# Projections packed as 128 columns and two 64-column halves, with a new order, in a four-layer kernel bound by TensorE

## The chip, the cores and the metric

The kernel runs on one core of a Trainium2 chip. The metric is the time of one execution in device microseconds (us). A kernel's time is the median of its runs; a profile describes one execution of its own.

## The reference

64 images of 96 channels and 28x28 pixels, in fp32, go through four layers in turn. Cut to what matters:

```python
# layer 0, B=64, C=96, HID=576, E=4 experts
rw   = softmax(relu(mean_hw(x) @ r_w1.T + r_b1) @ r_w2.T + r_b2)      # routing weights of an image
h    = silu(bn1(einsum('oc,bchw->bohw', exp_w, x)))                   # 96 -> 576
h    = silu(bn2(depthwise_5x5(h, einsum('be,eckl->bckl', rw, dw_w)))) # a kernel of its own for each image
h    = h * sigmoid(silu(mean_hw(h) @ se_w1.T + se_b1) @ se_w2.T + se_b2)
x    = x + bn3(einsum('boc,bchw->bohw', einsum('be,eoc->boc', rw, pw_w), h))   # 576 -> 96
# layers 1 and 3 (each with its own weights)
h    = relu(bn1(conv1x1(x, w1)));  h = relu(bn2(depthwise_3x3(h, wd)))
x    = x + bn3(conv1x1(h, w3))                                        # 576 -> 96
# layer 2, on the four 14x14 quadrants of an image
q    = group_norm(quadrants(x)); a = silu(conv1x1(q)); u = silu(depthwise_3x3(conv1x1(q)))
y    = selective scan of u in four directions, 16 states a channel
x    = x + channel_gate(a * group_norm(y))
```

The last step of layers 0, 1 and 3, 576 channels to 96 with the batch norm folded into the weights, is here called the projection.

## The kernel before

**Stages.** The images go through a software pipeline. One slot (`slot`) holds the scans of layer 2 for image t (`mamba`), layer 1 of image t+1, layer 0 of image t+2 and layer 3 of image t-1. There are 64 slots; `opening` comes before them and the last layer 3 after them.

**A convolution layer.** `expand` multiplies 96 channels to 576 in tiles of 128 channels (matmuls of 392 columns, L725; the last 64 channels as two 64-column matmuls, L755). ScalarE evicts each tile with batch norm and activation into one of two border tiles (L709), and a DMA from ScalarE's queue stores it to `ex` in DRAM (L742). A border tile can be filled again when its store has landed. `load` reads shifted rows back from `ex` into `rep` (SyncE's queue), `depthwise` runs the depthwise convolution as matmuls of 32 columns (L835), and ScalarE evicts into nine tiles `acc` of 128 partitions and 392 columns (L845). Such a tile g holds 64 channels; half of its partitions carry the even rows of the image (parity 0), half the odd rows (parity 1).

`project` sums over the nine tiles. There are two PSUM banks, one for each parity. The weights of a group g and a parity o are 96 columns whose rows of the other parity are zero, so that a group takes two matmuls over the same `acc` (L872), 18 in all. For layer 0 the weights `wp` are made for each image in `squeeze_excite`: matmuls mix the experts, and VectorE multiplies by the gate (L994). For layers 1 and 3 they are constants that `fold_bn3` scaled before the loop. VectorE then adds each bank and the bias to x in SBUF, one instruction for each parity (`add`, L876).

**Layer 2.** `head` normalizes (`group_norm`, whose matmuls are L1075, L1071 and L1072), projects (L1119, L1162) and runs the small convolution (L1141, L1173). `scans` has ScalarE make decays (L1269) and copy `du` (L1279, one buffer), VectorE make products (L1291) and scan them in two directions (L1296, L1301), GpSimd add and weigh them (L1248), and TensorE collect them into `y` (L1223). `tail` normalizes, gates and adds to x.

**The order.** The whole program is straight-line code. `Plan` collects operations with an engine, a cost in us, buffers, keys and a due time, and `run` places them one after another on modelled engines: among those that can start soon it takes the one with the earliest due time. The due times come from a slot's length T, from where an operation stands in its slot, and from a table of offsets, `DUE`, with one entry for each kind of operation. The result is one fixed order of instructions for each engine, and each engine runs its own in that order. The costs only decide the order, not what the chip does. Where TensorE would have been idle for long in the model, `idle` puts matmuls on zeros (L539) to keep its clock up. PSUM has four banks of the pool `ps`, one for `y`, one for `du` and two for the products.

Of the kernel before, what the change touches and what calls it, by code (L numbers as in the profile page):

```python
# [15 lines left out]
P = 128  # L16
C = 96
# [235 lines left out]
class Plan:  # L253
# [7 lines left out]
    LAND = 0.7  # L261
    ALONE = 130e3
# [60 lines left out]
    def run(self, start=0.0):  # L323
# [23 lines left out]
        while left:  # L347
# [42 lines left out]
            o.behind = None  # L390
# [82 lines left out]
class Kernel:  # L473
    T = 145.0
# [13 lines left out]
        wp=(1, [P, 2, NG, C]),  # L488
# [90 lines left out]
    def fold_bn3(self, row, w3):  # L579

        k = w3.shape[1]
        self.nc.vector.tensor_tensor(w3, w3, row.rearrange("p (a o) -> p a o", a=1).to_broadcast([P, k, C]), ALU.mult)
# [12 lines left out]
    def setup(self, fold, banks):  # L595
# [22 lines left out]
        for layer, c in ((1, c1), (3, c3)):  # L618
# [4 lines left out]
            self.fold_bn3(self.row_of(banks, s3, eye, f"fold_row{layer}"), c("w3"))  # L623
# [75 lines left out]
    def expand(self, d):  # L699
# [17 lines left out]
        for t in range(4):  # L717
# [3 lines left out]
            for h in range(2):  # L721
                ps = pl.buf("ps")

                def mm(ps=ps, t=t, h=h):
                    nc.tensor.matmul(  # L725
                        ps()[:, :HALF], w1[:, t * P : t * P + P], x[:, h * HALF : (h + 1) * HALF], start=True, stop=True
                    )

                pl.op(PE, 0.72, mm, r=d["keys"], w=[ps], after=[("pad", i, h)])
                pl.op(  # L730
                    ACT, 0.68, lambda ps=ps, t=t, h=h, pad=pad: evict(pad[:, :, 1 + 7 * h : 8 + 7 * h, 2:30], ps, t),
                    r=[ps], w=[("pad", i, h)], table=d["table"],
                )
# [37 lines left out]
        pl.op(ACT, 0.68, lambda: evict(pad[:, :, :, 2:30], ps, 4), r=[ps], w=["hpad"], table=d["table"])  # L771
# [14 lines left out]
    def load(self, d, u):  # L786
# [18 lines left out]
        if layer == 0:  # L805
            pl.op(POOL, 1.3, spread, r=[d["kern"]], w=[wd])
# [7 lines left out]
    def depthwise(self, d, u):  # L814
# [41 lines left out]
    def project(self, d):  # L856
# [3 lines left out]
        if d["layer"] == 0:  # L860
            wp = self.squeeze_excite(d)
            terms = lambda o, g: (wp()[:, o, g], accs[g]())
        else:
            w3, wp = d["c"]("w3"), "none"
            terms = lambda o, g: (w3[:, NG * o + g], accs[g]())
        banks = [pl.buf("ps") for o in range(2)]

        def mm(lo):
            for g in range(lo, lo + 3):
                for o in range(2):  # L870
                    w, a = terms(o, g)
                    nc.tensor.matmul(banks[o]()[:C, :HALF], w, a, start=(g == 0), stop=(g == NG - 1))  # L872

        def add(o):
            xs = d["x"].rearrange("c (r o w) -> c o r w", o=2, w=28)[:, o]
            nc.vector.scalar_tensor_tensor(  # L876
                xs, banks[o]()[:C, :HALF].rearrange("c (r w) -> c r w", w=28), d["b3"], xs, ALU.add, ALU.add
            )

        for lo in range(0, NG, 3):  # L880
            pl.op(PE, 0.67 * 6, lambda lo=lo: mm(lo), r=[*(accs[lo : lo + 3] if lo else accs), wp], w=banks)
        for o in range(2):
            pl.op(DVE, 0.65, lambda o=o: add(o), r=[banks[o], *d["keys"]], w=d["keys"])

    def routing(self, d):
# [6 lines left out]
        pl.op(DVE, 0.97, lambda: nc.vector.tensor_reduce(rw()[:C, 9:10], d["x"], AX.X, ALU.add), r=d["keys"], w=[rw])  # L892
# [5 lines left out]
            ACT, 0.35,  # L898
# [15 lines left out]
        pl.op(DVE, 0.6, top, w=[pt, rw])  # L914
        pl.op(ACT, 0.21, lambda: nc.scalar.activation(pt()[:, :E], pt()[:, :E], AF.Exp), w=[pt], table=EXP)

        def weights():
# [5 lines left out]
        pl.op(DVE, 0.75, weights, r=[pt], w=[rw])  # L923
        pl.op(
            ACT, 0.3, lambda: nc.scalar.activation(mix(), c("smask"), AF.Copy, scale=rw()[:, 10:11]), r=[rw], w=[mix]
# [7 lines left out]
        pl.op(ACT, 0.58, lambda: nc.scalar.copy(kern(), pk()[:96, :360]), r=[pk], w=[kern])  # L933

    def squeeze_excite(self, d):
# [16 lines left out]
        pl.op(ACT, 0.6, hidden, r=[ps], w=[sc], table=SILU)  # L952
# [27 lines left out]
        pl.op(DVE, 0.2, lambda: nc.vector.tensor_tensor(v(), ps()[:, 8 : 8 + NG], c("se_b2"), ALU.add), r=[ps], w=[sc])  # L980
# [8 lines left out]
        pl.op(ACT, 0.92, gate, w=[sc], table=SILU)  # L989
        for lo, hi, bank, acc in banks:  # L990
            for o in range(2):
                pl.op(
                    DVE, 0.58,
                    lambda o=o, lo=lo, hi=hi, acc=acc: nc.vector.tensor_tensor(  # L994
                        wp()[:, o, lo:hi],
                        acc(),
                        sc()[:, o * NG + lo : o * NG + hi].rearrange("p (g a) -> p g a", a=1).to_broadcast([P, hi - lo, C]),
                        ALU.mult,
                    ),
                    r=[sc, bank], w=[wp],  # L1000
                )
# [48 lines left out]
    def group_norm(self, key, imgs):  # L1050
# [23 lines left out]
        pl.op(DVE, 1.05, stats, r=key, w=[gs])  # L1074
        pl.op(PE, 0.25, lambda: nc.tensor.matmul(ps()[:C, :2], ones, mv()[:, :, 0], start=True, stop=True), r=[gs], w=[ps])  # L1075
        pl.op(ACT, 0.7, deviations, r=[ps], w=[gs])
        pl.op(PE, 0.4, second, r=[gs], w=[ps2])
        pl.op(ACT, 0.24, lambda: nc.scalar.activation(inv(), ps2()[:C, :2], AF.Identity, bias=self.eps), r=[ps2], w=[gs])
# [17 lines left out]
    def head(self, q):  # L1096
# [14 lines left out]
        pl.op(ACT, 1.1, norm, r=[gs, q["xkey"]], w=["hn"])  # L1111
# [21 lines left out]
        pl.op(ACT, 0.9, keep, r=banks, w=["p2"])  # L1133
        ps = pl.buf("ps")

        def taps(ps=ps):
# [14 lines left out]
            ACT, 0.6,  # L1151
# [14 lines left out]
            ACT, 0.6, lambda ps=ps: nc.scalar.activation(flat(a), ps()[:C, :HALF], AF.Silu, bias=c("p1_b")),  # L1166
# [10 lines left out]
        pl.op(ACT, 0.5, lambda: nc.scalar.copy(self.bc, ps2()[C:, :HALF]), r=[ps2], w=["bc"])  # L1177
        pl.op(ACT, 0.36, lambda: nc.scalar.dma_start(self.bcd[i2], self.bc), r=["bc"], w=[("bcd", i2)], nbytes=50176, land=2.2)
        pl.op(
            ACT, 0.58,  # L1180
# [3 lines left out]
        pl.op(POOL, 1.02, lambda: nc.gpsimd.tensor_tensor(inner(2), inner(0), u, ALU.mult), r=["dd0", q["ukey"]], w=["dd2"])  # L1184
        pl.op(
            POOL, 0.9,
# [16 lines left out]
    def scans(self, q, at):  # L1203
# [49 lines left out]
        for k in range(2):  # L1253
# [6 lines left out]
            for j in range(J):  # L1260
# [5 lines left out]
                def decay(fs=fs, d=dd[j], k=k, j=j):  # L1266
# [9 lines left out]
                pl.op(ACT, 1.88, decay, r=[dd[j]], w=[("decay", n)], table=EXP, due=at(i) - 9.0)  # L1276
                du = pl.buf("du")
                pl.op(
                    ACT, 0.5, lambda du=du, d=dd[j]: nc.scalar.copy(du()[:, :HALF], d()[:, 2]), r=[dd[j]], w=[du], due=at(i) - 3.0  # L1279
                )  # L1280
                for o in range(2):
# [4 lines left out]
                    def products(du=du, B=B, o=o):  # L1286
# [6 lines left out]
                    pl.op(DVE, 1.0, products, r=[du, B], w=["b"])  # L1293
                    pl.op(
                        DVE, 1.78,
# [4 lines left out]
                        DVE, 1.78,  # L1300
# [5 lines left out]
                    if not o:  # L1306
                        first = g
                        pooled(1.88, [h], g, ALU.add, h, g)
# [4 lines left out]
                    pooled(1.88, [h, g], yc, ALU.add, h, g, turned=True)  # L1313
                pooled(1.73, [first], yc, ALU.add, yc, first)
                pooled(1.88, [Cs], yc, ALU.mult, yc, c=Cs)
# [4 lines left out]
    def tail(self, q):  # L1320
# [6 lines left out]
            DVE, 0.65,  # L1327
# [11 lines left out]
        pl.op(ACT, 0.57, affine, w=[gs])  # L1339
# [13 lines left out]
        pl.op(ACT, 1.1, norm, r=[gs, q["ukey"]], w=[pa])  # L1353

        def gated():
# [4 lines left out]
        pl.op(DVE, 0.95, gated, r=[q["akey"], pa], w=[q["ukey"], cz])  # L1360
        pl.op(PE, 0.25, lambda: nc.tensor.matmul(pc()[:MID, :2], c("ca1"), cz()[:, :2], start=True, stop=True), r=[cz], w=[pc])
        pl.op(
            ACT, 0.25,
# [12 lines left out]
        pl.op(ACT, 0.58, sigmoid, r=[pd], w=[cz], table=EXP)  # L1376
# [12 lines left out]
        pl.op(DVE, 0.82, gate, r=[q["ukey"], cz], w=[q["xkey"]], lock=True)  # L1389
# [130 lines left out]
```

## Time and profile before

| | |
|---|---|
| median of 3 runs | 9306.1 us (9301.3 to 9313.9) |
| profiled execution, its time | 9312.2 us |
| its span, first to last instruction | 9310.4 us |
| TensorE busy | 8870.7 us (95%), mean granted clock 0.965 |
| VectorE busy | 7772.0 us (83%) |
| GpSimd busy | 6778.1 us (73%) |
| ScalarE busy | 6345.8 us (68%) |
| DMA engines, mean | 218 GB/s |

How to read the lines shown below. The page's first part gives for each engine its busy time, its share of the span and its instructions; PE is TensorE, PEld its weight loads, DVE VectorE, ACT ScalarE, POOL GpSimd, SP SyncE. A line of the view of stretches has the stretch in us from the start, its length, the busy time of PE, PEld, DVE, ACT and POOL with the number of instructions, the granted TensorE clock as a share of full speed, the busy share of the DMA engines, and GB/s. A line of a group has the source line, engine, operation, the tiles written and read, shapes and count, then busy us and mean ns of one, then the idle time of the engine just before them and what ended it. A line of the timeline has start, duration, engine, source line, operation and, in brackets, the idle time before it and what ended that. An fp32 matmul has two records. Line numbers are those of the kernel before; from L539 on, those of the kernel after are 5 to 17 higher.

### The profile page before, as it was taken

What the parts mean: (1) busy time and instruction counts of PE and PEld (TensorE: products, weight loads), DVE (VectorE), ACT (ScalarE), POOL (GpSimd) and SP (SyncE); (2) the same over time, 40 slices, a digit from 0 to 9 for tenths busy, and PEclk for the clock granted to TensorE, in tenths of its full rate; (3) what the DMA queues carried; (4) which work ended last, traced back from release to release, by engine and by line L of the source; (5) the groups of instructions that cost most, each with busy time, mean ns of one, the idle gap of its engine ahead of it and who ended that gap; (6) DMA issues with size and microseconds to landing.
All of it is one profiled execution on the core that took longest, in us unless ns stands there. A gap on an engine that the chain in (4) does not pass through costs nothing. (4 is left out here: it accounts for less than half of the span.)

```text
span 9310.4 us, 198515 instructions
## 1 busy us (share of the span) xinstructions
PE 8870.7 (95%) x78114; PEld 4120.6 (44%) x78114; DVE 7772.0 (83%) x7806; ACT 6345.8 (68%) x10934; POOL 6778.1 (73%) x4445
## 2 busy tenths in 40 slices
PE   7899999999999999999999999999999999999997
PEld 3344444444444444444444444444444444444443
DVE  1888888888888888888888888888888888888886
ACT  3667767767667677667677676676676676776763
POOL 2777777777777777777777777777777777777775
PEclk9899999999999999999999999999999999999998
DMA  6688888888888888888888888888888888888884
GB/s 174 185 213 231 223 220 225 227 222 220 224 226 219 221 229 221 215 229 224 219 225 227 223 222 225 224 220 222 228 221 222 227 222 215 230 223 220 225 227 105
DMA packets 1063983, 2029.93 MB, mean 218 GB/s; under 512 B 114065, under 2 KB 890001, under 8 KB 1062673
## 3 DMA queue, kind: packets, MB, share of 16 engines
q1 hardware_dynamic: 810576, 1520.44, 66.6%
q10 hardware_dynamic: 252480, 496.79, 15.4%
q8 instruction: 624, 10.22, 0.5%
q14 instruction: 303, 2.47, 0.1%
HBM read 1499.83 MB, written 516.95 MB: 217 GB/s over the span
## 5 line engine op out<-in xcount | busy, mean ns | idle before, releaser
L835 PE MATMUL ps<-rep,wd 64*32 64x392 f32 (+1 forms) x50688 | 3609.0, 521 | 38.8 <-DMA rep<-ex 14.9
L1301 DVE TENSOR_TENSOR_SCAN g<-decay,b 128x788 f32<-128x788 f32 x1536 | 2755.1, 1794 | 324.8 <-ACT decay L1269 190.1
L1296 DVE TENSOR_TENSOR_SCAN h<-decay,b 128x788 f32<-128x788 f32 x1536 | 2721.4, 1772 | 0.0
L835 PEld LDWEIGHTS ps<-rep,wd 64*32 64x32 f32 (+1 forms) x50688 | 1491.4, 110 | 1822.9 <-issue 1596.4
L1248 POOL TENSOR_TENSOR yc<-h,g 128x784 f32<-128x784 f32 x768 | 1436.9, 1871 | 1095.9 <-DVE h L1296 657.6
L1291 DVE TENSOR_TENSOR b<-du,B 128x784 f32<-128x784 f32 x1536 | 1505.0, 980 | 675.9 <-ACT du L1279 605.8
L845 ACT ACTIVATE acc<-ps,l_bn2b,l_bn2s 128x392 f32<-128x392 f32 x1728 | 1124.2, 674 | 1338.1 <-PE ps L835 1311.3
L1248 POOL TENSOR_TENSOR g<-h,g 128x784 f32<-128x784 f32 x768 | 1425.7, 1856 | 801.4 <-DVE h L1296 800.6
L872 PE MATMUL ps<-acc,blob 128*96 128x392 f32 x4608 | 1602.3, 498 | 4.7
L1248 POOL TENSOR_TENSOR yc<-yc,C 128x784 f32<-128x784 f32 x768 | 1426.5, 1857 | 55.2
L1269 ACT ACTIVATE decay<-dd,A 128x784 f32<-128x784 f32 x1536 | 1372.5, 943 | 38.0 <-DVE h L1296 14.4
L1248 POOL TENSOR_TENSOR yc<-yc,g 128x784 f32<-128x784 f32 x768 | 1318.1, 1716 | 45.9
L725 PE MATMUL ps<-x,blob 96*128 96x392 f32 x3072 | 1186.5, 518 | 22.3 <-ACT border L709 9.5
L709 ACT ACTIVATE border<-ps,l_bn1b,l_bn1s 128x392 f32<-128x392 f32 x1536 | 976.0, 677 | 220.0 <-DMA ex<-border 109.1
L872 PEld LDWEIGHTS ps<-acc,blob 128*96 128x96 f32 x4608 | 725.8, 163 | 755.8 <-issue 635.3
L588 POOL TENSOR_TENSOR wd<-kern,blob 96x640 f32<-96x640 f32 x576 | 753.6, 1317 | 163.1 <-PE ps L835 85.1
L1269 ACT ACT_TABLE_LOAD x439 | 563.2, 1283 | 334.7 <-issue 178.6
L725 PEld LDWEIGHTS ps<-x,blob 96*128 96x128 f32 x3072 | 536.7, 191 | 547.5 <-ACT acc L845 79.7
L872 PE MATMUL ps<-acc,wp 128*96 128x392 f32 x2304 | 771.8, 493 | 0.6 <-ACT a L1166 0.6
L872 PEld LDWEIGHTS ps<-acc,wp 128*96 128x96 f32 x2304 | 376.4, 163 | 383.7 <-issue 373.6
L1279 ACT COPY du<-dd 128x392 f32<-128x392 f32 x768 | 374.2, 487 | 219.0 <-DVE b L1291 124.3
L1223 PE MATMUL y<-yc,blob 128*32 128x392 f32 x3072 | 398.1, 502 | 29.8 <-POOL yc L1248 29.8
(144 smaller groups left out, 6599.8 us busy)
## 6 DMA issues: line engine op xcount, KB each, us to landing
rep<-ex SPq DMA_DIRECT2D x4032, 224.0 KB, 5.1
ex<-border ACTq DMA_DIRECT2D x512, 480.0 KB, 5.5
dd<-ddd SPq DMA_DIRECT2D x384, 588.0 KB, 7.2
ex<-border ACTq DMA_DIRECT2D x256, 512.0 KB, 5.1
B<-bcd SPq DMA_DIRECT2D x256, 392.0 KB, 4.3
C<-bcd SPq DMA_DIRECT2D x256, 392.0 KB, 4.8
wd<-taps SPq DMA_DIRECT2D x512, 192.0 KB, 6.7
ddd<-dd ACTq DMA_DIRECT2D x128, 441.0 KB, 3.5
```

Source lines behind the costliest of these rows:

```text
L588: self.nc.gpsimd.tensor_tensor(out, taps.rearrange("k (n a) -> k n a", a=1).to_broadcast([k, n, cb]), mask.rearrange("k (a c) -> k a c", a ...
L709: nc.scalar.activation(dst, ps()[:, :HALF].rearrange("p (r o w) -> p o r w", o=2, w=28), d["func"], bias=bias[:, t : t + 1], scale=scale[: ...
L725: nc.tensor.matmul(ps()[:, :HALF], w1[:, t * P : t * P + P], x[:, h * HALF : (h + 1) * HALF], start=True, stop=True)
L835: nc.tensor.matmul(ps()[32 * b : 32 * b + 32, :HALF], wd()[64 * h : 64 * h + lanes, at : at + 2 * CB], rep()[64 * h : 64 * h + lanes, b, : ...
L845: nc.scalar.activation(acc(), ps()[:, :HALF], d["func"], bias=bias[:, at : at + 1], scale=scale[:, at : at + 1], **kw)
L872: nc.tensor.matmul(banks[o]()[:C, :HALF], w, a, start=(g == 0), stop=(g == NG - 1))
L1223: nc.tensor.matmul(y()[32 * j : 32 * j + 32, :HALF], c("sel"), ys[j]()[:, 2 * u : 2 * u + 2], start=(k == 0 and u == 0), stop=(k == 1 and ...
L1248: nc.gpsimd.tensor_tensor(*vs, op)
L1269: nc.scalar.activation(fs[:, :, u, :, :SEQ], d()[:, :2].rearrange("p o (i l) -> p o i l", i=2), AF.Exp, scale=self.A[:, at : at + 1],)
L1291: nc.vector.tensor_tensor(out, v, w, ALU.mult)
L1296: lambda h=h, ff=ff: nc.vector.tensor_tensor_scan(flat(h()), ff, b, 0.0, ALU.mult, ALU.add),
L1301: lambda g=g, ff=ff: nc.vector.tensor_tensor_scan(flat(g())[:, ::-1], ff[:, ::-1], b[:, ::-1], 0.0, ALU.mult, ALU.add),
```

## The change

A group's two matmuls of 96 columns become one of 128 columns and two of 64 columns over half of the pixels each. The 128 columns hold all 96 outputs of parity 0 and the outputs 64 to 95 of parity 1. The outputs 0 to 63 of parity 1 are made by two matmuls of 64 columns and 196 pixels, which lie in the two column halves of the array and write the two halves of the second bank's partitions. VectorE adds four pieces to x in place of two: 96 and 32 partitions of the first bank, and twice 64 partitions of the second. The weights are packed to match: `w3` and `wp` have 192 columns for each group; the gating of parity 1 in layer 0 takes two instructions a bank, and the fold takes three instructions a layer in layers 1 and 3.

The order is planned anew. `T` goes from 145 to 134, the table `DUE` is another one, many modelled costs are lower (some are shown), and the model gives a result a short lag after its engine is free.

```diff
-    out = np.zeros((4, 2, CB, 2, NG, C), np.float32)
-    for o in range(2):
-        out[:, o, :, o] = w3.reshape(4, 2, CB, NG, C)[:, o]
-    p.add("w3", out.reshape(P, 2 * NG, C))
+    w3 = w3.reshape(4, 2, CB, NG, C)
+    out = np.zeros((4, 2, CB, NG, 2 * C), np.float32)
+    out[:, 0, :, :, :C] = w3[:, 0]
+    out[:, 1, :, :, C:P] = w3[:, 1, :, :, 64:]
+    out[:, 1, :, :, P:] = w3[:, 1, :, :, :64]
+    p.add("w3", out.reshape(P, NG, 2 * C))
...
 DUE = (
-    71, -2, 48, -17, 58, 181, 21, -12, 9, -37, -2, 21, 37, -23, 1, -16, 19, -12, 30, -17, 33, -40, 12, -8, -30, -60,
...
+    3, -600, 26, 3, -7, 47, 39, 26, 30, 0, -27, -34, 26, 4, 10, -8, 4, 15, 102, 0, 101, -7, -12, -94, -208, -19, -99,
...
+    LAG = {PE: 0.0, DVE: 0.1, ACT: 0.1, POOL: 0.05, SP: 0.0}
...
+            else:
+                end += lag
...
-                    d.ready = max(d.ready, end + (self.HOP[d.engine] if d.engine != e or o.nbytes else 0.0))
+                    d.ready = max(d.ready, end + (self.HOP[d.engine] if d.engine != e or o.nbytes else min(lag, 0.1)))
...
-    T = 145.0
+    T = 134.0
...
-        wp=(1, [P, 2, NG, C]),
+        wp=(1, [P, NG, 2 * C]),
...
-            self.fold_bn3(self.row_of(banks, s3, eye, f"fold_row{layer}"), c("w3"))
+            row = self.row_of(banks, s3, eye, f"fold_row{layer}")
+            for lo, hi, out in ((0, C, 0), (64, C, C), (0, 64, P)):
+                self.fold_bn3(row[:, lo:hi], c("w3")[:, :, out : out + hi - lo])
...
-                ACT, 0.88 if sums else 0.68, lambda ps=ps, acc=acc, h=h: evict(ps, u if sums else 2 * u + h, acc),
+                ACT, 0.67 if sums else 0.57, lambda ps=ps, acc=acc, h=h: evict(ps, u if sums else 2 * u + h, acc),
...
             for g in range(lo, lo + 3):
-                for o in range(2):
-                    w, a = terms(o, g)
-                    nc.tensor.matmul(banks[o]()[:C, :HALF], w, a, start=(g == 0), stop=(g == NG - 1))
+                w, a, kw = weights()[:, g], accs[g](), dict(start=(g == 0), stop=(g == NG - 1))
+                nc.tensor.matmul(banks[0]()[:, :HALF], w[:, :P], a, **kw)
+                for h in range(2):
+                    nc.tensor.matmul(
+                        banks[1]()[64 * h : 64 * h + 64, :SEQ], w[:, P:], a[:, h * SEQ : h * SEQ + SEQ], **kw
+                    )
...
+        def first():
+            add(xs(0), banks[0]()[:C, :HALF], 0, C)
+            add(xs(1)[64:], banks[0]()[C:, :HALF], 64, C)
+
+        def second():
+            for h in range(2):
+                add(xs(1)[:64, 7 * h : 7 * h + 7], banks[1]()[64 * h : 64 * h + 64, :SEQ], 0, 64)
+
         for lo in range(0, NG, 3):
-            pl.op(PE, 0.67 * 6, lambda lo=lo: mm(lo), r=[*(accs[lo : lo + 3] if lo else accs), wp], w=banks)
-        for o in range(2):
-            pl.op(DVE, 0.65, lambda o=o: add(o), r=[banks[o], *d["keys"]], w=d["keys"])
+            pl.op(PE, 3.0, lambda lo=lo: mm(lo), r=[*(accs[lo : lo + 3] if lo else accs), wp], w=banks)
+        pl.op(DVE, 1.02, first, r=[banks[0], *d["keys"]], w=d["keys"])
+        pl.op(DVE, 0.64, second, r=[banks[1], *d["keys"]], w=d["keys"])
...
+            def gated(o, lo=lo, hi=hi, acc=acc):
+                for a, b, out in ((0, C, 0),) if o == 0 else ((64, C, C), (0, 64, P)):
+                    v = sc()[:, o * NG + lo : o * NG + hi].rearrange("p (g a) -> p g a", a=1)
+                    nc.vector.tensor_tensor(
+                        wp()[:, lo:hi, out : out + b - a], acc()[:, :, a:b], v.to_broadcast([P, hi - lo, b - a]), ALU.mult
+                    )
...
-                pl.op(ACT, 1.88, decay, r=[dd[j]], w=[("decay", n)], table=EXP, due=at(i) - 9.0)
+                pl.op(ACT, 1.68, decay, r=[dd[j]], w=[("decay", n)], table=EXP, due=at(i) - 9.0)
...
-                    pl.op(DVE, 1.0, products, r=[du, B], w=["b"])
+                    pl.op(DVE, 0.9, products, r=[du, B], w=["b"])
```

More of the change, by code (lines that the diff above doesn't have):

```diff
@@ L389, in run @@
             free[e] = end = t + cost
-            o.behind = None
+            o.behind, lag = None, self.LAG[e]
             if o.lock:
@@ L805, in load @@
         if layer == 0:
-            pl.op(POOL, 1.3, spread, r=[d["kern"]], w=[wd])
+            pl.op(POOL, 1.27, spread, r=[d["kern"]], w=[wd])
         else:
@@ L897, in routing @@
         pl.op(
-            ACT, 0.35,
+            ACT, 0.25,
             lambda: nc.scalar.activation(
@@ L912, in top @@
             nc.vector.tensor_scalar(lg, lg, m, None, ALU.subtract)
-        pl.op(DVE, 0.6, top, w=[pt, rw])
-        pl.op(ACT, 0.21, lambda: nc.scalar.activation(pt()[:, :E], pt()[:, :E], AF.Exp), w=[pt], table=EXP)
+        pl.op(DVE, 0.52, top, w=[pt, rw])
+        pl.op(ACT, 0.13, lambda: nc.scalar.activation(pt()[:, :E], pt()[:, :E], AF.Exp), w=[pt], table=EXP)
         def weights():
@@ L921, in weights @@
             nc.vector.scalar_tensor_tensor(rw()[:, :4], lg, m, c("emask"), ALU.mult, ALU.mult, accum_out=rw()[:, 10:11])
-        pl.op(DVE, 0.75, weights, r=[pt], w=[rw])
+        pl.op(DVE, 0.55, weights, r=[pt], w=[rw])
         pl.op(
-            ACT, 0.3, lambda: nc.scalar.activation(mix(), c("smask"), AF.Copy, scale=rw()[:, 10:11]), r=[rw], w=[mix]
+            ACT, 0.27, lambda: nc.scalar.activation(mix(), c("smask"), AF.Copy, scale=rw()[:, 10:11]), r=[rw], w=[mix]
         )
@@ L932, in routing @@
         pl.op(PE, 0.65, kernels, r=[mix], w=[pk])
-        pl.op(ACT, 0.58, lambda: nc.scalar.copy(kern(), pk()[:96, :360]), r=[pk], w=[kern])
+        pl.op(ACT, 0.4, lambda: nc.scalar.copy(kern(), pk()[:96, :360]), r=[pk], w=[kern])
     def squeeze_excite(self, d):
@@ L950, in hidden @@
             nc.scalar.activation(sc()[:n4, 3 * NG + 1 :], c("zmask"), AF.Copy, scale=z())
-        pl.op(ACT, 0.6, hidden, r=[ps], w=[sc], table=SILU)
+        pl.op(ACT, 0.5, hidden, r=[ps], w=[sc], table=SILU)
         def excite():
@@ L987, in gate @@
                 nc.scalar.activation(sc()[:, o * NG : o * NG + NG], v(), AF.Identity, bias=par, scale=par)
-        pl.op(ACT, 0.92, gate, w=[sc], table=SILU)
+        pl.op(ACT, 0.82, gate, w=[sc], table=SILU)
         for lo, hi, bank, acc in banks:
-            for o in range(2):
[L992 to L1001, printed above, removed]
+            def gated(o, lo=lo, hi=hi, acc=acc):
[4 more added lines that the diff above has]
+                    )
+            for o in range(2):
+                pl.op(DVE, 0.52 + 0.1 * o, lambda o=o, gated=gated: gated(o), r=[sc, bank], w=[wp])
         return wp
@@ L1109, in norm @@
                 )
-        pl.op(ACT, 1.1, norm, r=[gs, q["xkey"]], w=["hn"])
+        pl.op(ACT, 0.9, norm, r=[gs, q["xkey"]], w=["hn"])
         banks = [pl.buf("ps"), pl.buf("ps")]
@@ L1131, in keep @@
             nc.scalar.copy(self.p2[:, 2], banks[1]()[:, :224])
-        pl.op(ACT, 0.9, keep, r=banks, w=["p2"])
+        pl.op(ACT, 0.7, keep, r=banks, w=["p2"])
         ps = pl.buf("ps")
@@ L1150, in head @@
         pl.op(
-            ACT, 0.6,
+            ACT, 0.5,
             lambda ps=ps: nc.scalar.activation(
@@ L1299, in scans @@
                     pl.op(
-                        DVE, 1.78,
+                        DVE, 1.7,
                         lambda g=g, ff=ff: nc.vector.tensor_tensor_scan(
@@ L1326, in tail @@
         pl.op(
-            DVE, 0.65,
+            DVE, 0.53,
             lambda: nc.vector.scalar_tensor_tensor(flat(u), flat(u), self.D4, q["y"]()[:C, :HALF], ALU.mult, ALU.add),
@@ L1351, in norm @@
                 )
-        pl.op(ACT, 1.1, norm, r=[gs, q["ukey"]], w=[pa])
+        pl.op(ACT, 0.9, norm, r=[gs, q["ukey"]], w=[pa])
         def gated():
@@ L1387, in gate @@
                 )
[L1389 removed]
+        pl.op(DVE, 0.64, gate, r=[q["ukey"], cz], w=[q["xkey"]], lock=True)
     def mamba(self, t, base, span, more):
```

59 lines of the change are left out of this document (29 added, 30 removed), and 8 rows, old and new, of the table DUE.

## The prediction

> **What bounds the kernel now.** I read the page first, then the busy time of three slots, then TensorE's groups with their idle time, then the timeline around the longest wait. Page and stretches:
>
> ```profile
> PE 8870.7 (95%) x78114; PEld 4120.6 (44%) x78114; DVE 7772.0 (83%) x7806; ACT 6345.8 (68%) x10934; POOL 6778.1 (73%) x4445
> ```
> ```profile
> 4620.04:4762.23 142.19, 137.38 (x1219) 64.11 (x1219) 120.60 (x122) 98.94 (x172) 105.47 (x69) 0.97 0.85 222
> 4762.23:4902.43 140.20, 136.15 (x1218) 63.56 (x1218) 119.72 (x121) 99.38 (x172) 105.53 (x69) 0.98 0.85 225
> 4902.43:5044.24 141.81, 136.12 (x1219) 63.15 (x1219) 123.03 (x123) 99.19 (x172) 105.50 (x69) 0.97 0.86 223
> ```
>
> The three stretches are one slot each (from one L1075 to the same one a slot later): 141.4 us, TensorE busy 136.6 of it, VectorE 121.1, GpSimd 105.5, ScalarE 99.2. TensorE is the bound, with 4.8 us idle a slot; VectorE has 20.3. But 136.6 is not all work: the clock column says 0.97. Where idle time and lost clock come from:
>
> ```profile
> L872 PE MATMUL ps<-acc,blob 128*96 128x392 f32 x4608 | 1602.3, 498 | 4.7
> ...
> L872 PE MATMUL ps<-acc,wp 128*96 128x392 f32 x2304 | 771.8, 493 | 0.6 <-ACT a L1166 0.6
> ...
> L1162 PE MATMUL ps<-hn,blob 96*96 96x392 f32 x256 | 115.1, 531 | 34.1 <-ACT p L1131 31.8 <-ACT acc L845 2.0 <-ACT p L1130 0.3
> ...
> L1075 PE MATMUL ps<-gs,blob 96*96 96x2 f32 x512 | 84.6, 235 | 228.7 <-ACT border L709 226.8 <-DVE gs L1063 1.9
> ```
> ```profile
> 4613.10 0.52 ACTq L742 DMA_DIRECT2D ex<-border  x1
> ...
> 4619.31 1.25 ACT L709 ACTIVATE border<-ps,l_bn1b,l_bn1s 128x392 f32<-128x392 f32 x2 [2.58 <-DMA ex<-border]
> ...
> 4620.04 0.48 PE L1075 MATMUL ps<-gs,blob 96*96 96x2 f32 x2 [4.63 <-ACT border L709]
> ```
> ```profile
> 4608.00:4615.30 7.30, 7.30 (x36) 3.27 (x28) 2.57 (x6) 5.69 (x9) 0.00 (x0) 1.00 1.04 255
> 4615.30:4620.00 4.70, 0.11 (x1) 0.00 (x0) 3.17 (x2) 2.12 (x4) 0.00 (x0) 0.90 0.73 254
> 4620.00:4628.70 8.70, 8.57 (x70) 5.07 (x74) 5.76 (x5) 5.18 (x12) 6.10 (x7) 0.50 0.86 247
> ```
>
> One knot a slot holds over half of TensorE's idle time. The expansion has two border tiles. ScalarE may fill one again only when its store to `ex` has landed (5.5 us at the median). The eviction at 4619.31 waits for that; the PSUM banks behind it stay full, and TensorE stands for 4.63 us. In the 8.7 us after it the granted clock is 0.50. So the knot costs twice: 226.8 us of waiting over the run, and by the clock column of the three slots 2.7% of 141.4 = 3.8 us a slot, 232 us over the 61 slots in which the view of waits counts it. [...]
>
> **The projections.** Durations from the timeline:
>
> ```profile
> 4078.31 4.19 PE L872 MATMUL ps<-acc,blob 128*96 128x392 f32 x12
> 4082.43 1.34 PE L1119 MATMUL ps<-hn,blob 97*32 97x224 f32 x24
> ...
> 4098.13 0.88 PE L755 MATMUL ps<-x,blob 96*64 96x392 f32 x4
> 4098.94 2.96 PE L725 MATMUL ps<-x,blob 96*128 96x392 f32 x8
> ...
> 4107.31 8.06 PE L872 MATMUL ps<-acc,blob 128*96 128x392 f32 x24
> 4115.21 1.15 PE L725 MATMUL ps<-x,blob 96*128 96x392 f32 x3
> ```
>
> Each fp32 matmul is two records, that is two passes. From 4107.31 to 4115.21 are 24 passes: 0.329 us each, and going from 96 columns to 128 costs nothing. The two 64-column matmuls of L755 (four records) take 0.81 us to the next start: they run side by side, two passes of 0.329, plus 0.15. The 12 passes of L872 ahead of the 32-column matmuls of L1119 take 4.12 instead of 3.95: plus 0.17. [...] With 128 columns the load is 0.03 longer (PEld 191 ns of L725 against 163 of L872).
>
> Before, a group g is two full-width matmuls: 4 x 0.329 = 1.32 us. After, it is one full-width matmul (0.66), a pair of 196 columns (2 x 0.165 = 0.33) and one way out and back (0.35): 1.34 us. The 0.33 us saved in streaming is paid back in switching, because `mm` alternates within every group. A projection stays at 12.0 us. Over 192 projections: +0.02 x 9 x 192 = +35 us at most. Counted over the whole order, changes of array width go from 2569 to 5763, and what other lines save in switches leaves about 0; I take +20.
>
> [...]
>
> **The other edits.** VectorE: two reads of 96x392 (L876, 616 ns) become two of 392 columns and two of 196 (nearest rows L1358 345 and L1380 404 ns): +0.75 us a projection. The gating of `wp` gets one more instruction a bank: 640 ns for 480 elements and 547 for 384 (L994) leave 0.17 us of fixed cost, +0.35 us a slot. Together 2.6 us a slot, 121.1 to 123.7, hidden under TensorE; what covers it is VectorE's 20.3 us of idle time. Fold: four more small VectorE instructions before the loop, under 2 us; ahead of the loop TensorE waits for constants anyway. Table loads of ScalarE go from 1077 to 1086 at 1.28 us: 12 us on an engine 68% busy, nothing. Warm-up matmuls on zeros (L539) go from 75 to 148, their columns from 31282 to 54548; now they take 71.3 us, so +53 if each costs its time, 0 if it only fills idle time. I take +27.
>
> **The order.** It decides. I counted TensorE's work between the expansion that fills a border tile and the next one that needs the same tile. Before, a slot has three such distances of 4.3 to 4.4 us and one of 7.3; the store alone takes 5.5, with evictions 7 to 8. After, the shortest is 4.9, the next 9.5. The stretch L725 x4, L1223, L725 x4, L1075 above becomes four expansions, then depthwise work, two, depthwise work, two. So the knot should open: -227 for the wait and -232 for the clock. The wait of L1162 for ScalarE's copy goes too, since it no longer stands just behind the matmuls whose copy it needs: -32.
>
> What comes instead: the order was planned with a projection at 9.0 us; the rows say 12.0. After each of three projections VectorE's queue stands about 3 us at the addition to x, with the next scans queued behind it, and the sums and collecting matmuls behind those: 9 us a slot. VectorE has 141.4 - 123.7 = 17.7 us to swallow it. New waits of TensorE: nothing, or as much as today's knot with its clock, 459 us. I followed one stretch by the rows. After the gating VectorE has four scans and a product (8.1 us) and GpSimd three steps (5.5 us) before the next collection; TensorE has the projection (12.0 us) and over 7 us more. That is 13.6 us against 19, so I am nearer the low end: a quarter of the 9 us, 2.3 us a slot, 143 us over 62 slots.
>
> Sum, from the profiled execution's own 9312.2 us (span 9310.4; 0.07% above the median of 9306.1): 9312 - 227 - 232 - 32 + 20 + 27 + 143 = 9011 us.
>
> **Rivals.** The knot moves: some other wait of 4 to 5 us a slot, again followed by half clock. For it: ScalarE's queue is full of waits for TensorE, and four PSUM banks are not many. Against it: the distances above. Price: 9312 + 20 + 27 - 32 = 9327 us; a wait a fifth shorter or longer gives 9235 to 9420.
>
> VectorE becomes the bound, and it is slower than before: the late projections stop VectorE, and its idle time, 605.8 us of it before L1291 for ScalarE's `du`, stays. 123.7 + 20.3 = 144.0 us a slot, +2.6 x 64: 9480 us. It decides once VectorE's idle time exceeds 17.7 us a slot. Against it: much of that idle time follows from the knot, where ScalarE stands as well.
>
> The changes of width cost nothing: 570 us less on TensorE, which would need 136.6 - 3.8 - 8.9 = 124 us a slot; then VectorE, 123.7 us and half of its idle time, holds the slot at 134: 9312 - 7.4 x 64 = 8840 us. Against it: rows with 0.15 to 0.17 us each way.
>
> **How the numbers follow.** Forecast, 8870 to 9170 us: 0.50. Knot moves: 0.20, of which by its prices about a third each is faster, the same and slower. VectorE bound: 0.20. Free switches: 0.10. Predicted is the likeliest, 9011. The range of 8 in 10 goes from 8780, somewhat under the free switches, to 9420, which leaves out most of the VectorE case and little else. A difference under 0.2% (19 us) cannot be told from none. Faster: 0.50 + 0.10 + 0.07, less 0.02 for the forecast's own tail: 0.65; same 0.07; slower 0.20 + 0.07 and that tail's rest, 0.28.
>
> **What would show it.** Right: a projection still takes some 12 us of TensorE, with starts about 1.34 us apart from group to group; the idle time before the group-norm matmul falls from 227 us to under 60; the clock rises from 0.965 to over 0.98; VectorE is 170 us busier. Wrong: groups 1.0 us apart (then the gain is TensorE's streaming); the clock still 0.97 or a new wait over 4 us in every slot (the knot moved); TensorE idle behind VectorE's scans (VectorE bound).

## The result and the profile after

The changed kernel takes 9620.7 us (median of 4 runs, 9610.5 to 9632.0) against 9304.3 (9301.3 to 9313.9) for the kernel before beside it: ratio 1.0339, 95% interval 1.0321 to 1.0356. Forecast were 9011 us and a range of 8780 to 9420. It is slower by 316 us, outside the range and of the other sign.

The page after, first part (busy time, share of the span 9608.6 us, instructions):

```profile
PE 9005.7 (94%) x81716; PEld 3726.0 (39%) x81716; DVE 7970.1 (83%) x8322; ACT 6355.8 (66%) x10943; POOL 6785.0 (71%) x4445
```

VectorE is 198 us busier (170 forecast), TensorE 135 us. The clock is 0.966, as before. TensorE's groups with their idle time (busy, mean ns of one, idle before, what ended it):

```profile
L842 PE MATMUL ps<-rep,wd 64*32 64x392 f32 (+1 forms) x50688 | 3671.3, 515 | 318.7 <-DMA rep<-ex 154.4 <-DMA wd<-taps 72.5 <-ACT acc L852 59.1
...
L877 PE MATMUL ps<-acc,blob 128*128 128x392 f32 x2304 | 1090.9, 556 | 4.6
L879 PE MATMUL ps<-acc,blob 128*64 128x196 f32 x4608 | 645.4, 359 | 0.0
...
L1179 PE MATMUL ps<-hn,blob 96*96 96x392 f32 x256 | 110.5, 513 | 3.1 <-ACT border L716 2.1 <-DVE x L886 1.0
...
L1092 PE MATMUL ps<-gs,blob 96*96 96x2 f32 x512 | 79.4, 225 | 1.5 <-ACT border L716 0.8 <-ACT acc L852 0.4 <-DVE gs L1080 0.3
```

The two waits that were to go have gone: the group-norm matmul (L1075 before, L1092 now) stands 1.5 us in place of 228.7, the one at L1162 (now L1179) 3.1 in place of 34.1. (A later matmul of the group norm, L1071 before and L1088 now, stands 42.0 us in place of 9.5.) The depthwise matmul (L835, now L842) has taken their place: 318.7 us of idle time against 38.8. Groups of a projection, in the timeline (start, length):

```profile
4106.56 0.93 PE L877 MATMUL ps<-acc,blob 128*128 128x392 f32 x2
4107.42 0.55 PE L879 MATMUL ps<-acc,blob 128*64 128x196 f32 x4
4107.90 0.93 PE L877 MATMUL ps<-acc,blob 128*128 128x392 f32 x2
```

One group starts 1.34 us after the other, as forecast: packing as such saves TensorE next to nothing here. Four successive slots (stretch, us, busy time of PE, PEld, DVE, ACT, POOL, granted clock, DMA share, GB/s; a slot from here on runs from one squeeze matmul, L962, to the next slot's):

```profile
3281.34:3423.43 142.09, 135.20 (x1277) 56.00 (x1274) 124.06 (x130) 99.14 (x171) 105.69 (x69) 1.00 0.82 223
3423.43:3575.45 152.02, 144.23 (x1278) 58.80 (x1275) 124.19 (x130) 99.83 (x171) 105.60 (x69) 0.93 0.77 208
3575.45:3717.64 142.19, 135.15 (x1278) 55.96 (x1275) 124.18 (x130) 99.03 (x171) 105.68 (x69) 1.00 0.82 222
3717.64:3868.63 150.99, 143.27 (x1277) 59.12 (x1275) 124.30 (x130) 99.61 (x171) 105.62 (x69) 0.94 0.77 208
```

The same work takes 142 us in a slot whose clock stays up and 151 to 152 in one with 17 to 20 us at half clock.

I added up the trace for slots 5 to 60, in us per slot ("at half clock" is busy time at a granted clock of 0.50, "work" is TensorE's busy time less half of that):

| kernel | slot | TensorE idle | at half clock | work |
|---|---|---|---|---|
| before | 141.5 | 4.75 | 7.7 | 132.9 |
| changed | 145.7 | 7.04 | 7.3 | 135.0 |
| packing alone | 145.7 | 6.85 | 13.1 | 132.3 |
| order alone | 144.3 | 5.36 | 7.8 | 135.1 |
| before, with a fill | 141.4 | 3.20 | 5.2 | 135.6 |
| before, free ring | 139.2 | 3.03 | 5.2 | 133.6 |
| changed, in turns | 139.5 | 7.76 | 7.4 | 128.0 |
| changed, in turns, fills | 137.4 | 4.53 | 2.2 | 131.8 |
| changed, fills | 143.2 | 3.75 | 1.0 | 139.0 |

The rows below "changed" are the experiments that follow; a fill, matmuls on zeros, counts as work.

### The profile page after: what moved, and what is told of

It is laid out like the page before. It is cut to its first block, busy times and chain, and to the rows that moved or that the text cites. A ratio compares the mean times of both kernels' runs of the same rounds, so it can differ in the third digit from the quotient of the medians.

```text
span 9608.6 us, 205828 instructions
## 1 busy us (share of the span) xinstructions
PE 9005.7 (94%) x81716; PEld 3726.0 (39%) x81716; DVE 7970.1 (83%) x8322; ACT 6355.8 (66%) x10943; POOL 6785.0 (71%) x4445
## 5 line engine op out<-in xcount | busy, mean ns | idle before, releaser
L842 PE MATMUL ps<-rep,wd 64*32 64x392 f32 (+1 forms) x50688 | 3671.3, 515 | 318.7 <-DMA rep<-ex 154.4
L842 PEld LDWEIGHTS ps<-rep,wd 64*32 64x32 f32 (+1 forms) x50688 | 1305.6, 108 | 2305.6 <-issue 1720.3
L732 PE MATMUL ps<-x,blob 96*128 96x392 f32 x3072 | 1278.5, 545 | 67.7 <-ACT acc L852 43.1
L877 PE MATMUL ps<-acc,blob 128*128 128x392 f32 x2304 | 1090.9, 556 | 4.6
L886 DVE SCALAR_TENSOR_TENSOR x<-ps,l_bn3b,x 64x196 f32<-64x196 f32 (+2 forms) x768 | 401.0, 522 | 681.1 <-PE ps L877 668.3
L732 PEld LDWEIGHTS ps<-x,blob 96*128 96x128 f32 x3072 | 574.4, 203 | 664.6 <-issue 279.4
L1098 POOL TENSOR_TENSOR gs<-gs,mhalf 96x2 f32<-96x2 f32 x256 | 179.2, 700 | 665.3 <-ACT gs L1095 655.2
L879 PE MATMUL ps<-acc,blob 128*64 128x196 f32 x4608 | 645.4, 359 | 0.0
L877 PE MATMUL ps<-acc,wp 128*128 128x392 f32 x1152 | 528.1, 540 | 0.0
L879 PEld LDWEIGHTS ps<-acc,blob 128*64 128x64 f32 x4608 | 230.5, 136 | 666.4 <-issue 586.7
```

The lines of the kernel that those rows point to most:

```text
L732: nc.tensor.matmul(ps()[:, :HALF], w1[:, t * P : t * P + P], x[:, h * HALF : (h + 1) * HALF], start=True, stop=True)
L842: nc.tensor.matmul(ps()[32 * b : 32 * b + 32, :HALF], wd()[64 * h : 64 * h + lanes, at : at + 2 * CB], rep()[64 * h : 64 * h + lanes, b, : ...
L877: nc.tensor.matmul(banks[0]()[:, :HALF], w[:, :P], a, **kw)
L879: nc.tensor.matmul(banks[1]()[64 * h : 64 * h + 64, :SEQ], w[:, P:], a[:, h * SEQ : h * SEQ + SEQ], **kw)
```

## The experiments

**The two halves of the change, and grouping.** Packing alone: the new weights, matmuls and reads, with the order of before on every engine.

> The new packing alone, in the order of the kernel before (same DUE, T and costs; ScalarE's, GpSimd's and SyncE's instructions stand exactly as before). Theory A, the loss comes from the order and the packing is about neutral on TensorE (a group 1.34 us against 1.32): 9310 to 9400 us, TensorE's wait of 3.7 us a slot at the group-norm matmul still there. Theory B, the packing itself loses (switches, four pieces on VectorE instead of two): 9500 us or more, with the new idle time of TensorE behind the pieces.

Measured: 9560.2 us, ratio 1.0271 (1.0255 to 1.0286), clock 0.947. Its waits of TensorE (us in total, times, longest):

```profile
PE ps L1089 <- ACT border L713: 231.1, 61, 5.1
PE ps L729 <- DVE x L883: 138.8, 61, 2.9
```

The knot at the group norm is untouched and a second wait has come: the expansion after layer 1's projection needs a PSUM bank that VectorE has yet to read. One slot's timeline, VectorE's rows and then TensorE's, and the stretch behind it (columns as above):

```profile
4491.17 1.79 DVE L1310 TENSOR_TENSOR_SCAN h<-decay,b 128x788 f32<-128x788 f32 x1
4493.05 0.98 DVE L1305 TENSOR_TENSOR b<-du,B 128x784 f32<-128x784 f32 x1
4493.94 2.15 DVE L883 SCALAR_TENSOR_TENSOR x<-ps,l_bn3b,x 96x392 f32<-96x392 f32 x4
...
4495.35 0.90 PE L729 MATMUL ps<-x,blob 96*128 96x392 f32 x2 [2.32 <-DVE x L883]
```
```profile
4496.40:4506.60 10.20, 10.20 (x38) 3.24 (x35) 6.28 (x12) 7.04 (x9) 7.82 (x6) 0.50 0.62 204
```

The four additions take 2.15 us and stand behind a scan and a product. TensorE waits 2.32 us, and then runs at 0.50 for 10.2 us.

Order alone: the changed kernel with the old weights, matmuls and reads.

> The new order alone, with the projections packed as before. Theory A: about the time of the changed kernel, 9560 to 9680 us, with TensorE waiting some 4.8 us a slot for loads of rep and wd. Theory B: near the kernel before, 9250 to 9350 us.

Measured: 9532.3 us, 1.0242 (1.0226 to 1.0259). Both halves are slower by themselves, by 247 and 219 us; together they cost 316, so they overlap. By the table the packing loses through waits and half clock, the order mainly through 2.2 us more of work a slot.

Grouping: in each operation of three groups, first the three full-width matmuls, then the three pairs, so that the array changes width once out and back for three groups.

```diff
-            for g in range(lo, lo + 3):        # full width g, pair g, full width g+1, ...
+            for g in range(lo, lo + 3): full(g)
+            for g in range(lo, lo + 3): pair(g)
```

The code is shortened. In the old order:

> The new packing in the old order, but within each operation of three groups the three full-width matmuls come first and the three pairs after them: 3 ways out and back a projection in place of 9. If a way costs 0.35 us, a projection takes 9.9 us instead of 12.0, 403 us less of TensorE over 192 projections. Theory A: 8880 to 9050 us if TensorE is the bound in this order. Rival: the knot at the border tiles and VectorE hold the slot, 9200 us or more, and TensorE's idle time grows by what it saves.

In the new order:

> The same grouping in the new order; a projection then takes 9.9 us where the order was planned with 9.0. Theory A1, the new waits come from projections that run 3 us longer than planned: they shrink with the gap, and the time falls by more than the 403 us of TensorE, to 8850 to 9050 us. Theory A2, the waits lie in the order itself (loads of rep too close behind the stores of ex): they stay, about 7 us a slot, and the time is 9180 to 9300 us.

Measured: 9668.0 us, 1.0387 (1.0371 to 1.0402), in the old order; 9259.5, 0.995 (0.9933 to 0.9967), in the new. TensorE's work falls by 4.9 us a slot in the old order and 6.3 in the new (6 ways out and back less in each of 3 projections at 0.35 us make 6.3): the price of a switch holds in the new order, and within a quarter in the old. What becomes of it depends on the order. In the old one the knot grows from 231.1 to 350.6 us and the clock drops to 0.924: less work for TensorE there only means more waiting.

**Is VectorE's reading hidden?** The kernel before with its own matmuls, and only the two additions cut into the four pieces of the changed kernel (code shortened).

```diff
-            add(xs, banks[o]()[:C, :HALF])
+            cuts = ((0, C, 0, 14),) if o == 0 else ((64, C, 0, 14), (0, 64, 0, 7), (0, 64, 7, 14))
+            for lo, hi, r0, r1 in cuts: add(xs[lo:hi, r0:r1], banks[o]()[lo:hi, 28*r0:28*r1])
```

> The kernel before with its own matmuls and its own order on every engine; only VectorE's two additions into x after each projection are cut as in the changed kernel (one of 96 rows, one of 32 rows, two of 64 rows and half the columns). Theory V (VectorE's 2.6 us more per slot are not hidden, because VectorE is the engine that frees the projection's banks): most of what the packing alone lost comes back without the packing, 9313 + 150 to 250 = 9460 to 9560, with TensorE waiting for VectorE's additions at the expansion after layer 1's projection (139 us in the packing alone) and a second stretch at half clock in each slot. Rival S (the loss belongs to the new column widths on TensorE): 9313 within 30, no such wait.

Measured: 9490.4 us, 1.019 (1.0175 to 1.0206). Waits of TensorE:

```profile
PE ps L725 <- DVE x L880: 57.5, 61, 1.9
PE ps L932 <- DVE x L880: 33.5, 58, 0.6
```

The pieces by themselves cost 180 us in the old order, where the whole packing costs 247, although VectorE is busy only 83% of the time. Its idle time lies elsewhere in the slot than the additions that a bank waits for. What makes the other 67 was not tried.

The packing alone again, with zeros for TensorE ahead of the expansion before that wait:

```diff
+                    if d["layer"] == 0 and t == 3 and h == 0:
+                        self.idle(ps(), 2.2)
```

> The packing alone in the old order, with 2.2 us of matmuls of zeros put ahead of the expansion that runs just before the wait for VectorE's additions (in a bank that this expansion overwrites). Theory C (a wait of 2.3 us at this place brings 10.2 us at half clock with it): the second stretch at half clock is gone, busy time at half clock falls from 13.1 to about 8 us per slot, 9560 - 64 x 2.6 = 9390 (9370 to 9420). Rival W (only the wait itself costs, the half clock has another cause): 9560 within 30. The fill adds nothing if it only replaces the wait.

Measured: 9439.7 us, 1.0136 (1.0121 to 1.0151): 120 us less. The wait for VectorE's additions falls from 138.8 to 5.8 us and half clock from 13.1 to 7.8 us a slot. TensorE spends the time of the wait on zeros instead, so what came back is the clock (the 5.3 us a slot would be 170 us at half their length).

**What was the knot worth?** The same kind of fill in the kernel before, ahead of the wait at the group norm (layer 1, t 3, h 1).

> The kernel before with 2.2 us of matmuls of zeros ahead of layer 1's expansion of tile 3, second half, which is the last TensorE work before the wait at the group-norm matmul (L1075). Nothing else is moved. Theory C (the half clock follows from the wait): one stretch of 6.8 to 7.7 us at half clock per slot goes, 64 x 3.4 to 3.8 = 215 to 245 less, about 9085 (9060 to 9130), clock in the page above 0.98. Rival W (the clock falls there for another reason): 9313 to 9350, clock still 0.965. Rival D (the fill delays the border evictions that the wait is for): the wait stays, up to 64 x 2.2 = 140 more, 9450.

Measured: 9309.1 us, 0.9998 (0.9988 to 1.0007): nothing, though half clock fell from 7.7 to 5.2 us a slot by the record and the wait from 226.8 to

```profile
PE ps L1077 <- ACT border L709: 105.7, 60, 3.3
```

The wait's end stayed where it was, 37.3 and 37.5 us into the slot in the mean: it is set by the store's landing (36.5), not by TensorE. And behind it the work runs no faster: from there to L1162 it took 27.1 us before and 26.7 with the fill. What comes first there are the group norm's small matmuls with ScalarE between them; that this is the reason was not tested.

The kernel before, with the stores to `ex` reading a tile of weights instead of the border tiles, so that no border tile waits for its store to land (the expansion is then left out of what the projections get; code shortened):

```diff
-                src, dst = (... for v in (pad, ex[P * t : P * t + P]))
+                src, dst = (... for v in (const, ex[P * t : P * t + P]))
```

> The kernel before, order and work as they are, but the stores of the expanded border tiles to ex read a constant tile of weights in place of the border tile, so that no border eviction has to wait for a store to land (what is stored is not the expansion: the projections' inputs are left out of the computation). It does alone what the prediction's first two terms claimed for the change. Theory P (the prediction: the wait at the group-norm matmul, 227 us, goes and 232 us of half clock with it): 9310 - 459 = 8850, clock above 0.98. Theory Q (after the run with the fill: the half clock after the wait belongs to the small matmuls too, and is worth about 2 us per slot at most): 9310 - 227 - (0 to 130) = 8955 to 9085. Rival N (something else is next late, so the wait only moves): above 9150, with a new wait of over 1.5 us per slot.

Measured: 9156.7 us, 0.9842 (0.9827 to 0.9858): 148 us less, where the prediction's first two terms said 459. Its waits:

```profile
PE ps L836 <- ACT gs L1079: 68.5, 48, 3.3
PE ps L1076 <- ACT border L709: 39.9, 61, 0.9
```

187 us of waiting go and 68.5 come back at once: with the knot open, the group norm's chain on ScalarE is late next.

**Where the new wait for `rep` comes from.** The changed kernel, loading `rep` from DRAM tiles that no store ever writes in the loop.

```diff
-            src = d["ex"][ch + 64 * h : ...]
+            src = self.still[k][ch + 64 * h : ...]
```

> The changed kernel, order and work as they are, but the loads of rep read tiles in DRAM that are written once at the start, in place of ex, so that no load has to wait for a store to land (what is computed after the expansion is not the reference's). Theory R (the trip of a store out to ex and of the load back is what the new order runs into): the wait for rep (154 us) falls below 40 us, and with it the half clock behind it (3.4 us per slot, 64 x 1.7 = 110): 9620 - 115 - 110 = 9395 (9360 to 9510). Rival N (another wait takes its place, the one for wd or for the evictions): within 60 of 9620.

Measured: 9657.2 us, 1.0379 (1.0358 to 1.04). The wait did not go, so my theory R, a trip of the data through DRAM, falls (in this run the loads bring nothing of the expansion). TensorE's and SyncE's waits:

```profile
PE ps L849 <- DMA rep<-still: 140.1, 51, 4.3
...
SPq L796 <- DMA ex<-border: 1739.3, 496, 18.3
```

Loads that read nothing of `ex` still wait for stores to it. In the changed kernel's timeline the first store is issued on ScalarE's queue, and 3 us later the load that TensorE misses on SyncE's:

```profile
4480.11 0.53 ACTq L749 DMA_DIRECT2D ex<-border  x1
...
4483.13 0.30 SPq L789 DMA_DIRECT2D rep<-ex  x1
...
4486.77 2.05 PE L842 MATMUL ps<-rep,wd 64*32 64x392 f32 x17 [2.45 <-DMA rep<-ex]
```

The store lands at 4483.11. Over slots 5 to 60 this load, the fourth of its unit, is issued 0.02 us after that landing at the median, in this kernel and in the one with the still tiles alike; with the order alone it is issued 5.5 us ahead of it. The semaphore numbers in the traces say why. In them the DMAs of SyncE and ScalarE tell of their landing through eight semaphores (100 and 102 to 108 in the changed kernel), and none was issued before the DMA that had its semaphore last had landed (7121 of 7121 successive pairs in the changed kernel, and as many with the order alone). The planned order of both kernels is the same, but the numbering is not: here the load draws the semaphore of that store (number 108 for both of the DMAs shown), with the order alone that of another DMA. The wait for `rep` is 154 us here and 40 with the order alone.

Then I told the planner that stores land 1.5 us later (5.0 and 4.7 for 3.5 and 3.2), in the grouped kernel below:

> The changed kernel with the projection's matmuls grouped in turns (9205 us), and the planner told that the stores to ex land 1.5 us later than it was told before (5.0 and 4.7 us for 3.5 and 3.2), so that it lays out another order with more room between a store and the load of it. Theory R (the planner's landing time is what is wrong in the new order): the wait for rep falls from 219 us to below 80, 9205 - 140 to 200 = 9000 to 9065. Rival (the due times were found for the old landing time, and another order of the same due times loses elsewhere): 9200 or above.

Measured: 10571.0 us, 1.1357 (1.1338 to 1.1376), clock 0.887. The due times belong to the costs that they were found for; another order from the same due times is far worse, and this run says nothing on the landing time.

**Grouped in turns, and fills.** The changed kernel's order with three full-width matmuls, three pairs, three pairs, three full-width, three full-width, three pairs.

> The changed kernel, order and reads as they are, with the projection's matmuls grouped: three of 128 columns, three pairs, then the next three pairs, three of 128 columns, then three of 128, three pairs. Two switches out and back fewer than with each three in the same turn count as one out and back per projection: 3 x 0.35 us per slot below the grouping by three (9259): 9259 - 67 = 9192, 430 below the changed kernel. Rival (what is saved on TensorE comes back as waits for loads and half clock, as in the old order): 9240 to 9280 or above.

Measured: 9204.9 us, 0.9874 (0.9854 to 0.9894). The switch's price holds once more (55 us below grouping by three, 67 expected; its runs spread over 43). Its waits for `rep` are 218.7 us. Zeros ahead of two units that wait, in the bank that the unit overwrites:

```diff
+            if (d["layer"], u) == (3, 3): self.idle(banks[0](), 2.0)
+            if (d["layer"], u) == (1, 4): self.idle(banks[0](), 1.2)
             for dx in range(k):
```

> The changed kernel with the projection's matmuls grouped in turns (9205 us), and matmuls of zeros ahead of two depthwise units that wait for their loads in each slot, in the bank that the unit then overwrites: 2.0 us ahead of unit 3 of layer 3 (wait for rep, 2.7 us in slot 30), 1.2 us ahead of unit 4 of layer 1 (wait for wd, 1.8 us). Order and work else as they are. Slots of this kernel that differ in their time at half clock differ in their period by 0.5 us for each us of it. Theory C (behind these waits comes dense depthwise work, so keeping TensorE busy through them keeps its clock): half clock falls from 7.4 to about 3 to 5 us per slot, 9205 - 64 x 1.2 to 2.2 = 9065 to 9130. Rival F (as with the fill in the old order, the clock is low for another reason or the fills delay the work behind them): 9195 or above.

Measured: 9104.0 us, 0.9781 (0.9764 to 0.9798), clock 0.982: 101 us less, and faster than both kernels. The same fills in the changed kernel as it is:

> The changed kernel as it is (9620 us), with matmuls of zeros ahead of two depthwise units in each slot: 2.0 us ahead of unit 3 of layer 3, 1.2 us ahead of unit 4 of layer 1. The waits themselves are not shortened. Theory C (the half clock behind these waits costs half its time): 7.3 us of half clock fall to about 3, 9620 - 64 x 1.5 to 2.2 = 9480 to 9525. Rival F (the half clock lies elsewhere, or the fills delay): 9600 or above.

Measured: 9482.5 us, 1.0184 (1.0167 to 1.0202), clock 0.985: 138 us less. Half clock falls from 7.3 to 1.0 us a slot, half of which would be 202 us; so some 138 us of the changed kernel's loss are half clock behind these waits. Dense depthwise work follows the wait here, small matmuls in the old order's knot, which fits the difference between the two fills but was not tested by itself.

**The pieces in the new order.** Order alone with the four additions.

> The new order with the old matmuls (9532 us), and VectorE's additions into x cut into the four pieces of the changed kernel; nothing else. Theory V (the pieces are what the packing costs in this order too): 9532 + 60 to 110 = 9590 to 9640. Rival S (the new order was planned with the pieces' costs, 1.02 and 0.64 us, so they are hidden in it, and the 88 us belong to the matmuls of two widths): 9532 within 25.

Measured: 9556.1 us, 1.0266 (1.0247 to 1.0285), against 1.0242 (1.0226 to 1.0259) without them: not told apart. In this order, planned with their costs, the pieces are hidden as far as 24 us between the medians can tell, and most of the 88 us of packing on top of it is not theirs. By the table these 88 us, 1.4 a slot, are TensorE's idle time (5.36 to 7.04) and not its work (135.1 and 135.0), and the wait that grew is the one for `rep` (40 to 154 us; 56 with the four additions, where the load draws the same semaphore as with the order alone).

## Why the prediction was wrong, point by point

By slot, forecast against measured (the table): the wait of the group norm -3.6 against -3.7; the one at L1162 -0.5 against -0.5; half clock -3.6 against -0.2 (0.4 us less of it, at half price); new waits +2.2 against +6.5 (idle 7.0, less what was left of 4.75 after those two); switching and fills +0.7 against +2.2 of work. Sum -4.8 against +4.3; the slot grew by 4.2, which makes 269 us in 64 slots, of the 298 between the two profiled executions.

- **A group costs what it did: right.** 1.34 us measured as forecast (in the trace before, records of 128 columns (L725) start 0.33 us apart, at 4099.38 and 4099.71, as those of 96 do), and its price of a switch, 0.35 us out and back (0.15, 0.17 and 0.03 of the prediction's rows), carried both kernels grouped in the new order to within some 40 us.
- **"So the knot should open: -227 for the wait": right in place, wrong in worth.** Both waits went. But this wait was worth only what the next late chain left: with the ring free and all else as before, both terms together brought 148 us, not 459.
- **"-232 for the clock": wrong step.** I tied the half clock to this one wait. After the change it is 7.3 us a slot in place of 7.7, behind other waits. In the old order the clock's record also overstated the price: a third less of it by the fill brought nothing.
- **New waits booked at their length alone: wrong.** The sum takes 143 us for them, with no half clock behind them. That was my assumption, and no run shows it: with the packing alone a wait of 2.32 us was followed by 10.2 us at 0.50, and filling it brought 120 us. The trace of the kernel before could have told me. One of its knots, and the stretch behind it:

```profile
4338.51 0.33 PE L1075 MATMUL ps<-gs,blob 96*96 96x2 f32 x2 [2.35 <-ACT border L709]
```
```profile
4338.00:4346.00 8.00, 7.20 (x62) 4.22 (x66) 7.76 (x6) 5.22 (x13) 3.72 (x6) 0.58 0.87 268
```

Over slots 5 to 60 the 55 waits at the knot were 1.9 to 5.4 us long, and half clock of 6.8 or 10.2 us came with every one of them (it began during the wait or within 2.6 us of its end). Elsewhere it differs between nearly the same waits: of the 55 at the expansion with the packing alone (2.1 to 2.9 us) 42 were and 13 were not, and two of the four slots of the changed kernel shown above have none.

- **"a quarter of the 9 us" of new waits: the largest miss.** I put them down to late projections on VectorE. VectorE's queue did stand as forecast (668.3 us at the addition to x, 3.5 us a projection), and the new order swallowed it. The new waits are for loads and for evictions, at the depthwise units. I had counted the distances between border tiles, and none between a unit's loads and its matmuls, nor what SyncE's loads wait for besides their data. Measured are 6.5 us a slot of new waits, not 2.3.
- **"hidden under TensorE" for VectorE's 2.6 us: wrong in the old order (180 us), right in the new one as far as could be told.** The rival "VectorE becomes the bound" came nearest in time (9480) but not in cause; "the knot moves" had the mechanism and too low a price.
- **Work +1.5 us above forecast** comes with the order (it is there without the packing). Of the order's 2.2 us a slot, 0.6 are matmuls on zeros, for which the prediction took half of their price (+27 us; L544 is busy 129.4 us against 71.3, so +58). The depthwise matmuls of 64 rows take 1.6 more, the collecting ones (L1240) 0.9, all others together 0.9 less. In part this is waiting shown as busy: in the kernel in turns, four records of a depthwise run that waits for an eviction take 1.04 us with 0.19 shown as idle; undisturbed, eight take 0.34. How much of the rest is that stays open. So does why the semaphores are numbered otherwise in the changed kernel, and whether a load that draws a luckier one would by itself bring back the 88 us: neither was tried.

## What to carry to other kernels

Removing a wait can be worth far less than its length, if another chain is late just behind it (187 us of waiting gone here, 68.5 back at once): before booking it, look for the next thing in the same stretch that ends late, and count a wait that ends with a DMA's landing from that landing. A share of busy time does not hide an operation (two more additions on VectorE, 83% busy, cost 180 us here in the old order): find the bank or buffer that its end sets free, and who needs it next. Where tiles of two widths alternate, try grouping by width (here 361 us less in the new order, 108 more in the old), and where dense work waits for a load, look at the granted clock behind the wait: filling two such waits with matmuls on zeros brought 101 and 138 us here.

## What the runs showed of the hardware that I had not expected

- In the kernel before, TensorE's clock stood at 0.50 for 6.8 or 10.2 us with each of 55 waits of 1.9 to 5.4 us; in the changed kernel it comes and goes from slot to slot with hardly changed waits, and by the four slots shown 17 to 20 us of it make a slot 9 to 10 us longer.
- Of two kernels with the same order and nearly the same work one waits 114 us more for `rep`. In it the load that TensorE misses shares a completion semaphore with a store, is issued 0.02 us after that store's landing, and is so even when it reads nothing that was stored.
